# Two buffers instead of four for the gathered rows of a message-passing kernel

## The chip, the cores and the metric

The kernel runs on one core of a Trainium2 chip. The metric is the device time of one launch in microseconds (us). Before the change it is 5778.92 us, the median of three runs (5755.6 to 5812.79).

## The reference

One layer of a graph network with 12,500 nodes and 400,000 edges, all in float32, edges sorted by destination. A node has 160 numbers: 64 scalars `s` and 32 three-vectors `v`. Cut to what matters:

```python
h_s = s @ lin1_ws * a * _inv(S_IN)                  # per node
h_v = einsum('nci,cd->ndi', v, lin1_wv) * a * ...
hid = silu(edge_scalars @ fc_w1 * _inv(R))          # per edge
w1, w2, w3, w4, w5 = split(hid @ fc_w2 * ..., ...)  # 224 weights per edge
es, ev = h_s[edge_src], h_v[edge_src]               # the gather
m_s1 = w1 * es * e0;   m_s2 = w4 * einsum('eci,ei->ec', ev, e1) * ...
m_v1 = (w2 * es)[:, :, None] * e1;  m_v2 = w3 * ev * e0;  m_v3 = w5 * cross(ev, e1) * ...
agg  = segment_sum(concat(...), edge_dst)           # per node again
out  = layernorm(x + gate(self_connection + agg @ lin2))
```

## The kernel before

**Stages.** A first stage (to about 115 us in the profile) computes the node table `h = [h_s, h_v]` and stores it as `h_tab` in HBM, 640 bytes a row. The long middle stage runs over the edges. A tile is 128 edges, one in each partition; there are 3125 tiles. Five tiles make a block (625 of them), whose messages go to a window of 32 destination nodes. Twenty tiles make a chunk, which is worked off in five steps of four tiles, called quads here. There are 782 steps: 780 of four tiles, then one of four and one of one tile. After a short end nothing is left: the node outputs are worked off between the steps.

**One step `n`** of the loop at the end (line 607 on) does this:

- `hide(n + 1)`: at every chunk's first step, SyncE loads the edge scalars `es` of the chunk (line 278, 320 KB in two transfers, two buffers); TensorE then multiplies them into `ph` (L290) and ScalarE applies SiLU into `hid` (L292).
- `gather(deep, ...)`: GpSimd issues one indirect DMA for each of the four tiles (L299). Each brings 128 rows of `h_tab`, 80 KB, into a quarter of the tile `hg`. The addresses are a column of `idx`, which SyncE loads for 125 tiles at a time (L466), as it does the edge attributes `eat` (L468).
- `weights`: TensorE makes the 224 weights of each edge in PSUM, `pw` (L311), in two buffers.
- `products`: VectorE multiplies `pw` by `hg` into `pr`: one instruction at L319, then three at L328. L319 is the first that needs the gathered rows, the last L328 the last one that reads them. `pr` has two buffers.
- Still on VectorE: one finished block is added to the node sums `acc` (L387), and the selection matrices of a later block are made, `oh` (L338) and `sel` (L341).
- `now`: for a pair of blocks that was finished in an earlier step, TensorE transposes (L369), ScalarE copies (L370), and for every eighth block TensorE applies the second linear map (L378).
- `sum_up` of the step before: TensorE sums the messages of four tiles into `pa` with 16 small matmuls (L357). A pair of finished blocks is copied out by ScalarE (L361).

**Order.** TensorE, VectorE, ScalarE and GpSimd execute in the order in which this loop is written; SyncE's order is a scheduler's. [...] GpSimd has nothing to do in the middle stage but gathers, so it runs ahead of the others, until no buffer of `hg` is free.

**Where the buffers come from.** `hg` is the only tile of the pool `deep`, and a pool with `bufs=k` hands out k buffers in turn. So the first gather of step n waits until the last L328 of step n-4 has read that buffer:

```python
    def gather(pool, idx):
        hg = pool.tile([P, Q, D], F32, name="hg")
        for t, i in enumerate(idx):
            nc.gpsimd.indirect_dma_start(
                out=hg[:, t, :], out_offset=None, in_=h_tab,
                in_offset=bass.IndirectOffsetOnAxis(ap=i, axis=0))
        return hg
```

A buffer of `hg` is 4 tiles of 160 float32, 2.5 KB in each partition. A loop at the end of the program that repeats the work for wide blocks uses the same pool; on these data it runs zero times.

Of the kernel before, what the change touches and what calls it, by code (L numbers as in the profile page):

```python
# [64 lines left out]
def gnn_kernel(  # L65
# [76 lines left out]
    with tc.tile_pool(name="nodes", bufs=2) as nodes, tc.tile_pool(  # L142
        name="nodes_ps", bufs=8, space=PSUM
# [310 lines left out]
    with tc.tile_pool(  # L454
        name="fin", bufs=1
    ) as fin, tc.tile_pool(name="edge", bufs=2) as edge, tc.tile_pool(
        name="deep", bufs=4
    ) as deep, tc.tile_pool(name="pw_ps", bufs=2, space=PSUM) as pw_ps, tc.tile_pool(
        name="pa_ps", bufs=2, space=PSUM
    ) as pa_ps, tc.tile_pool(name="misc_ps", bufs=2, space=PSUM) as misc_ps:  # L460
# [268 lines left out]
```

## Time and profile before

| | |
|---|---|
| median of three runs | 5778.92 us |
| the profiled execution | 5669.53 us, span of its instructions 5667.7 us |
| mean granted TensorE clock in it | 0.816 |
| middle stage | 781 steps from 120.8 to 5626.3 us, 7.05 us a step |
| TensorE / VectorE / GpSimd / ScalarE busy | 74% / 47% / 54% / 14% of the span |
| gathers (L299) | 3125, median 946 ns each, with 0.30 us between two of a quad |

A row of the table of groups names a source line, the engine, the operation, what it writes and reads, how often, its busy time and the mean duration, and then how long the engine stood idle just before such instructions and what ended most of that. A row of the list of waits says: engine and line, what it waited for, total us, times, longest us. A row of the timeline says: start, duration, engine, line, what it writes and reads, how many instructions were merged, and in brackets the idle time before and what ended it. "issue" there is time in which nothing that the profile shows was waited for; "remote" is an end that the profile can't assign to an instruction. The end of a matmul in the trace is modelled, not observed, so the "busy" of TensorE isn't a measure of how full it is.

### The profile page before, as it was taken

How to read it: one execution, taken by the hardware profiler on the slowest of the kernel's cores; microseconds unless marked ns; L12 is line 12 of the kernel's file. 1: busy time of each engine (PE TensorE's matmuls, PEld its weight loads, DVE VectorE, ACT ScalarE, POOL GpSimd, SP SyncE). 2: the span in 40 equal slices, each digit the busy share in tenths (PEclk: the TensorE clock that was granted, in tenths of full speed). 3: DMA queues.
4: the chain of work that ended last, by engine and by line, in shares of the span. 5: the costliest groups of instructions: out<-in, count | busy, mean ns of one | idle time of the engine just before them, and what ended most of it. 6: DMA issues, size and time to landing. Idle time of an engine off the chain costs nothing.

```text
span 5667.7 us, 89792 instructions
## 1 busy us (share of the span) xinstructions
PE 4182.8 (74%) x36179; PEld 2227.6 (39%) x36179; DVE 2642.3 (47%) x5628; ACT 809.3 (14%) x1639; POOL 3051.9 (54%) x3134
## 2 busy tenths in 40 slices
PE   6777777767777767777777777777776767777776
PEld 5334433333344434334333333433333433434343
DVE  4444444444444444444444444444444444444444
ACT  0111111111111111111111111111111111111111
POOL 3555555555555555555555555555555555555553
PEclk7788887888888878888888788887887888888787
DMA  6222222222222222222222222222222322232221
GB/s 172 68 72 73 72 72 66 73 74 65 76 76 67 74 68 74 74 70 74 72 74 73 63 76 69 73 77 68 75 72 63 82 67 73 71 79 69 68 69 46
DMA packets 232392, 416.39 MB, mean 73 GB/s; under 512 B 64580, under 2 KB 160592, under 8 KB 231713
## 3 DMA queue, kind: packets, MB, share of 16 engines
q0 software_dynamic: 150000, 256.20, 17.3%
q1 hardware_dynamic: 65972, 142.43, 9.9%
q10 hardware_dynamic: 15994, 11.93, 0.8%
q8 instruction: 285, 4.67, 0.3%
q14 instruction: 141, 1.16, 0.1%
HBM read 394.32 MB, written 16.00 MB: 72 GB/s over the span
## 4 chain that ended last, share of the span: by engine, by line
PE 31%; another core or an unknown queue 8%; issue 6%; DVE 3%; ACT 3%; DVEq 0%; DMA 0%; POOL 0%; ACTq 0%; POOLq 0%
PE pa L357 13%; PE pw L311 6%; PE ph L290 4%; PE po L378 3%; PE pt L369 2%; DVE pr L328 2%; ACT tt L370 1%; PE pa L348 1%; ACT hid L292 1%; DVE pr L319 0%; PE pp L406 0%; PE psc L510 0%; ACT L292 0%; DVEq L582 0%
## 5 line engine op out<-in xcount | busy, mean ns | idle before, releaser
L299 POOL DMA_INDIRECT hg<-h_tab,idx x3125 | 3029.5, 969 | 2562.8 <-DVE pr L328 962.0
L357 PE MATMUL pa<-pr,sel 128*32 128x192 f32 x25000 | 1813.8, 395 | 312.7 <-issue 298.8
L319 DVE TENSOR_TENSOR pr<-pw,hg 128x512 f32<-128x512 f32 x782 | 539.1, 689 | 2648.7 <-remote 1400.2
L357 PEld LDWEIGHTS pa<-pr,sel 128*32 128x32 f32 x25000 | 888.3, 127 | 1060.3 <-issue 768.8
L328 DVE TENSOR_TENSOR pr<-pw,hg 128x384 f32<-128x384 f32 x2346 | 1158.2, 549 | 5.7 <-issue 4.9
L311 PE MATMUL pw<-w,hid 64*128 64x224 f32 x6250 | 990.0, 429 | 48.3 <-issue 38.8
L369 PE MATMUL pt<-ident,sa 128*96 128x128 f32 x1250 | 317.8, 344 | 814.6 <-ACT tt L370 418.6
L311 PEld LDWEIGHTS pw<-w,hid 64*128 64x128 f32 x6250 | 645.2, 219 | 585.8 <-issue 530.2
L341 DVE TENSOR_TENSOR sel<-oh,eat 128x640 f32<-128x640 f32 x625 | 517.8, 828 | 168.2 <-PE pw L311 51.2
L290 PE MATMUL ph<-es,w 128*128 128x512 f32 x940 | 552.0, 673 | 10.8 <-issue 8.3
L369 PEld LDWEIGHTS pt<-ident,sa 128*96 128x96 f32 x1250 | 124.7, 144 | 1000.5 <-ACT tt L370 496.0
L361 ACT COPY sa<-pa 128x384 f32<-128x384 f32 x313 | 149.5, 478 | 2085.0 <-PE pa L357 1042.7
L292 ACT ACTIVATE hid<-ph 128x512 f32<-128x512 f32 (+1 forms) x470 | 247.0, 526 | 1242.9 <-PE ph L290 855.1
L378 PE MATMUL po<-tt,l 96*96 96x256 f32 (+1 forms) x1738 | 401.7, 383 | 9.6 <-issue 8.7
L378 PEld LDWEIGHTS po<-tt,l 96*96 96x96 f32 x1738 | 274.5, 164 | 127.1 <-issue 47.6
L370 ACT COPY tt<-pt 96x256 f32<-96x256 f32 x626 | 229.3, 366 | 588.0 <-PE pt L369 361.1
L290 PEld LDWEIGHTS ph<-es,w 128*128 128x128 f32 x940 | 165.8, 219 | 198.1 <-issue 184.7
L406 PE MATMUL pp<-ident,acc 96*128 96x96 f32 x196 | 44.9, 325 | 239.6 <-DVE acc L387 218.9
L338 DVE TENSOR_TENSOR oh<-rel,iota 128x160 f32<-128x160 int16 x625 | 196.3, 314 | 0.0
L382 ACT COPY os<-po 96x512 f32<-96x512 f32 (+1 forms) x79 | 45.6, 577 | 714.9 <-PE po L378 485.1
L387 DVE TENSOR_TENSOR acc<-acc,os 96x64 f32 x625 | 132.7, 212 | 12.6 <-ACT os L382 7.9
L406 PEld LDWEIGHTS pp<-ident,acc 96*128 96x128 f32 x196 | 23.8, 170 | 273.3 <-issue 187.5
(61 smaller groups left out, 794.7 us busy)
## 6 DMA issues: line engine op xcount, KB each, us to landing
es<-in_es_t_dram SPq DMA_DIRECT2D x312, 320.0 KB
hg<-h_tab,idx POOLq DMA_INDIRECT x3125
h_tab<-ht ACTq DMA_DIRECT2D x8, 960.0 KB
xt<-in_x_dram SPq DMA_DIRECT2D x24, 320.0 KB
out_dram<-y SPq DMA_DIRECT2D x24, 320.0 KB
eat<-in_ea_dram SPq DMA_DIRECT2D x25, 250.0 KB
xv<-in_xv_t_dram SPq DMA_DIRECT2D x25, 187.5 KB
xs<-in_xs_t_dram SPq DMA_DIRECT2D x25, 125.0 KB
```

Of the source, the lines that this page charges most:

```text
L290: nc.tensor.matmul(ph[:k, c], w1[:k, :k], es[:k, t0 * P + c0 * P:t0 * P + c1 * P], start=True, stop=True)
L292: nc.scalar.activation(hid[:k, c], ph[:k, c], AF.Silu, scale=1.0 / math.sqrt(64))
L299: nc.gpsimd.indirect_dma_start(out=hg[:, t, :], out_offset=None, in_=h_tab, in_offset=bass.IndirectOffsetOnAxis(ap=i, axis=0))
L311: nc.tensor.matmul(pw[:, t, :NWT], hid[r, c * P:(c + 1) * P], w2[r], start=True, stop=True)
L319: nc.vector.tensor_mul(pr[:, :n, 6 * V:10 * V].rearrange("p t (k c) -> p t k c", k=2), pw[:, :n, :2 * S].rearrange("p t (k c) -> p t k c", ...
L328: nc.vector.tensor_mul(bass.AP(tensor=full.tensor, offset=full.offset, ap=[full.ap[0], full.ap[1], [step * V, 3], [1, V]]), pw[:, :n, None ...
L338: nc.vector.tensor_tensor(oh, r[:, :, None].to_broadcast([P, TB, W]), iota[:, None, :].to_broadcast([P, TB, W]), op=OP.is_equal)
L341: nc.vector.tensor_mul(sel, oh[:, :, None, :].to_broadcast([P, TB, 4, W]), e[:, :, :, None].to_broadcast([P, TB, 4, W]))
L357: nc.tensor.matmul(pa[k * W:(k + 1) * W], sel[:, t, k], a, start=start, stop=stop)
L369: nc.tensor.transpose(pt[:, half, b], sa[:, b, half * V3:(half + 1) * V3], ident)
L370: nc.scalar.copy(tt[:, half, :, at_b:at_b + nb].rearrange("c k b n -> c b k n"), pt[:, half, :nb].rearrange("c b (k n) -> c b k n", k=4))
L378: nc.tensor.matmul(po[:, k, :nb], l2[:, terms[to, part, half]], tt[:, half, part, :nb], start=(n == 0), stop=(n == len(of) - 1))
```

## The change

The pool of the gathered rows has two buffers instead of four. Nothing else is edited.

```diff
     with tc.tile_pool(
         name="fin", bufs=1
     ) as fin, tc.tile_pool(name="edge", bufs=2) as edge, tc.tile_pool(
-        name="deep", bufs=4
+        name="deep", bufs=2
     ) as deep, tc.tile_pool(name="pw_ps", bufs=2, space=PSUM) as pw_ps, tc.tile_pool(
```

The first gather of step n now waits for the last L328 of step n-2. In the built program the instructions of TensorE, VectorE, ScalarE and GpSimd stand in the same order as before. On GpSimd the waits are attached otherwise: before, each gather of a quad waited for the landing of the gather eight places earlier, and the quad's first one also for VectorE; now the first one carries all of this (four landings and VectorE), and the other three wait for nothing. On SyncE, eight of the 25 loads of `idx` stand behind the `es` load of one more chunk, and a few loads of `idx`, `eat`, `xt` and stores of the output have changed places.

## The prediction

> **What bounds the kernel now.** I read the page's busy shares first, then the groups of L299 and L319, then the list of waits, then the timeline of GpSimd and VectorE side by side.
>
> ```profile
> PE 4182.8 (74%) x36179; PEld 2227.6 (39%) x36179; DVE 2642.3 (47%) x5628; ACT 809.3 (14%) x1639; POOL 3051.9 (54%) x3134
> ...
> L299 POOL DMA_INDIRECT hg<-h_tab,idx x3125 | 3029.5, 969 | 2562.8 <-DVE pr L328 962.0
> ```
>
> ```profile
> DVE pr L319 <- remote: 1400.2, 267, 19.1
> ...
> DVE pr L319 <- PE pw L311: 784.7, 285, 10.1
> ...
> DVE pr L319 <- DMA hg<-h_tab,idx: 16.9, 2, 16.6
> ```
>
> ```profile
> PEld pa L357 <- DVE pr L328: 23.6, 48, 1.2
> ...
> PE pa L357 <- DVE pr L328: 6.6, 17, 0.9
> ```
>
> No engine is full by its busy share. The waits say who is last: VectorE's product (L319) waits 2,649 us in all, for TensorE or for "remote", and for gathered rows only twice, both at the start. TensorE in turn hardly waits for products: 30 us in all (23.6 + 6.6). So in the middle stage TensorE's own chain sets the pace of 7.05 us a step. VectorE follows it with slack, and GpSimd follows VectorE: 962.0 us of its idle time end with the release of a buffer at L328. The doubt is "remote", 1400.2 us: could these be gathers? The timeline answers:
>
> ```profile
> 2498.34 0.95 POOL L299 DMA_INDIRECT hg<-h_tab,idx  x1 [3.96 <-DVE pr L328]
> ...
> 2503.35 0.95 POOL L299 DMA_INDIRECT hg<-h_tab,idx  x1 [0.31 <-issue]
> ...
> 2513.20 0.94 POOL L299 DMA_INDIRECT hg<-h_tab,idx  x1 [5.16 <-DVE acc L387]
> ```
>
> ```profile
> 2511.46 1.47 DVE L328 TENSOR_TENSOR pr<-pw,hg 128x384 f32<-128x384 f32 x3
> ...
> 2513.69 0.69 DVE L319 TENSOR_TENSOR pr<-pw,hg 128x512 f32<-128x512 f32 x1 [0.62 <-PE pw L311]
> 2514.37 1.49 DVE L328 TENSOR_TENSOR pr<-pw,hg 128x384 f32<-128x384 f32 x3
> ...
> 2524.64 0.69 DVE L319 TENSOR_TENSOR pr<-pw,hg 128x512 f32<-128x512 f32 x1 [7.49 <-remote]
> ...
> 2530.28 0.69 DVE L319 TENSOR_TENSOR pr<-pw,hg 128x512 f32<-128x512 f32 x1 [2.25 <-PE pw L311]
> ...
> 2538.71 0.69 DVE L319 TENSOR_TENSOR pr<-pw,hg 128x512 f32<-128x512 f32 x1 [3.33 <-PE pp L406]
> ```
>
> The product that ends at 2512.93 (2511.46 + 1.47) frees a buffer, and 0.27 us later GpSimd starts the quad for the product four steps on, at 2538.71. Counting back, the quad of 2498.34 belongs to the product at 2524.64, which waited 7.49 us for "remote"; its rows had been ordered by 2503.04, some 20 us earlier. So "remote" isn't the gather. The prefetch is far deeper than its latency needs.
>
> [...]
>
> ```profile
> 117.74 0.95 POOL L299 DMA_INDIRECT hg<-h_tab,idx  x1 [0.30 <-issue]
> ...
> 120.78 0.69 DVE L319 TENSOR_TENSOR pr<-pw,hg 128x512 f32<-128x512 f32 x1 [16.60 <-DMA hg<-h_tab,idx]
> ```
>
> From 118.69 to 120.78 are 2.1 us; the second product, which started at 125.39 behind a gather row that ended at 123.69, gives 1.7.
> [...] I use the trace's 1.7 to 2.1.
> [...] Gathers here take 940 to 1591 ns with a median of 946 and a mean of 969[...].
> [...] The trace shows half-clock stretches (0.50 in 2519.82 to 2530.05 us, 1.00 in 2482.28 to 2495.92)[...].
>
> **The change, part by part.**
>
> *1. The wait at the first gather: release by step n-2 instead of n-4.* Behind it on GpSimd are only later gathers; who waits for them is L319, and everything behind that on VectorE. From release to usable rows a quad takes 0.27 us, plus 4.70 (three times 1.25 and 0.95, the quad of 2498.34), plus 1.7 to 2.1: **6.7 to 7.1 us**. What is available is the time from the end of one product to the start of the second after it, on average two steps less one product: 2 x 7.05 - 2.17 = 11.9 us. Checked in the window: the product at 2524.64 would have its quad started at 2513.20 and usable at 2520.0, 4.6 us early; that at 2530.28 would be served behind it (start 2518.2, usable 2525.0), 5.3 early; that at 2538.71, released at 2526.82, would be usable at 2533.9, 4.8 early. GpSimd's own rate is no bound: 5.0 us a quad against 7.05.
>
> The mean isn't enough, since steps are uneven. Taking the interval for all 780 pairs from the timeline of L319 and L328: median 11.8, lowest twentieth below 7.9, lowest hundredth below 6.0, least 3.7 us (the last step of one tile). The tight ones are where TensorE's backlog has let three products come close, as at 668.01, 670.25 and 674.84: the last starts only 4.64 us after the first has ended at 670.20. Passing all products through the two-buffer rule in order, with the durations of this trace, makes 18 of them late with 1.7 us of landing, 26 with half a us more; by 2.8 us at most, **15 to 27 us** together. If VectorE's idle time before the next products takes this back, 2 to 3 us remain at the end; if nothing does, 15 to 26. I take most of it as regained, because TensorE needs a product only one step later, behind the next `pw` and the sums of the step before, and its waits for products are the 30 us above: **+4 us**, ends 0 and +27.
>
> *2. The waits gathered on the quad's first instruction.* Three or four more semaphore waits, whose rows on GpSimd's queue are 17 ns each: at most 0.07 us a quad, 53 us in all, beside 2,563 us of GpSimd idle. If it came after the release it would add 0.07 to the 6.7, inside the half us tried above. Without waits the other three gathers keep their 0.30 us spacing, as the first eight did at 115 to 123 us, which had none either. **0**.
>
> *3. SyncE's order.* Eight `idx` loads stand one `es` load later. That for group 7 now follows the load for chunk 39, which can start when chunk 37's scalars have been read (step 188); its first gather is that of step 217, released at step 215: 27 steps, some 190 us, cover a 62.5 KB load. Each `idx` load also waits until the gathers of the group before last have been issued, now two steps (14 us) later, with `eat`, `xt` and `es` queued behind it. The next `es` load is free to start only about five steps after the last one (35 us), so its own wait covers this. If that cover failed, 25 times 14 us would be on SyncE, and `ph` would be late. **0**, upper bound a few us each.
>
> *4. Below nothing?* No instruction leaves TensorE, VectorE or ScalarE, gathers start at the same releases as before, so DMA traffic falls in the same places. I see no gain beyond the clock's wandering.
>
> Sum: 5669.5 + 4 = 5673.5 us for the profiled execution, +0.07%. It lies 1.9% below the median of the runs shown (5778.92), so I carry the ratio over: **5783 us**.
>
> **The rivals.**
> - *Two quads are too few* (slower). If a quad needs 2 us more than 6.7[...], GpSimd's 5.0 + 2 us reach the step of 7.05 and lateness no longer heals: the same pass gives 55 us (idle taken back) to 222 us, with 2.5 us 435 or more. With 1 us it is still only 4 to 46, so it decides from about 2 us on. Against it: the gathers' narrow durations, and the two landings seen. [...] Middle: +140 us, **5920**.
> - *The gathers collide less* (faster). Later fetches might fall beside fewer other transfers, and TensorE's clock might be granted more. The windows of 1000 us differ between 0.81 and 0.83, so 1% is conceivable: **5720**. Against it: point 4.
> - *The change does nothing, because no more than two quads were ahead anyway*: **5779**. Ruled out as a reading by the 20 us above, but its time is the forecast's.
>
> **How the numbers follow.** Within 1% is about what a measurement here can tell from no change (the three runs spread by 1%). Forecast and the last rival 0.77, too few quads 0.17, of which nearly all above 1%, faster 0.06. So faster 0.06, same 0.77, slower 0.17. The range: the forecast with 0 to +27 us and the runs' own spread of half a per cent gives 5745 to 5830; I stretch it up to 5860 for the near end of the slower case (5834 to 6000).
>
> **What will show it.** Right: L319's wait for `hg` stays under some 40 us; the gathers' rows end some 4 to 6 us before the product's start, less landing, instead of 20; GpSimd's idle ends about as before, at L328; TensorE's waits for products stay near 30 us. Wrong: L319 waiting for `hg` by hundreds of us, gathers longer than 1 us on average, or `ph` waiting for `es`.

## The result, and the profile after

| | before, four buffers | after, two buffers |
|---|---|---|
| median of 12 runs | 5790.27 us | 5798.77 us |
| range | 5755.60 to 5812.79 us | 5774.58 to 5819.40 us |
| ratio, with its 95% interval | | 1.0018 [0.9997, 1.0038] |
| profiled execution | 5669.53 us | 5819.40 us |

The change cost about 0.2%, 8.5 us, and the interval touches no change. The two profiled executions must not be compared by their spans: that of the kernel before lies 1.5% below the lowest of its own 12 timed runs, and that of the kernel after is the highest of its. What can be compared is who waited for whom. One later execution of the two-buffer kernel took 11758 us, at a granted clock of 0.54; the ratio of its group below leaves it out. The waits of L319 and of GpSimd in the profile after:

```profile
DVE pr L319 <- remote: 1562.7, 287, 8.2
POOL hg L299 <- DVE pr L328: 1050.3, 299, 5.4
...
DVE pr L319 <- PE pw L311: 711.0, 261, 9.7
...
DVE pr L319 <- DMA hg<-h_tab,idx: 34.8, 9, 14.6
```

VectorE waited for gathered rows 34.8 us instead of 16.9, of which 14.6 are the first product. Five products take nearly all of the rest, 3.8 us each; one of them, with the gathers of its quad:

```profile
1541.63 0.68 DVE L319 TENSOR_TENSOR pr<-pw,hg 128x512 f32<-128x512 f32 x1
...
1548.77 0.69 DVE L319 TENSOR_TENSOR pr<-pw,hg 128x512 f32<-128x512 f32 x1 [3.77 <-DMA hg<-h_tab,idx]
```

```profile
1541.85 0.95 POOL L299 DMA_INDIRECT hg<-h_tab,idx  x1 [3.52 <-DVE acc L387]
...
1544.36 1.46 POOL L299 DMA_INDIRECT hg<-h_tab,idx  x1 [0.30 <-issue]
```

The product before last had started at 1539.40, only 2.23 us ahead of the last one, and released the buffer at 1541.59; the rows were usable 7.19 us later. All five look like this: two products 2.1 to 2.2 us apart, then 7.2 to 7.3 us from the release to the next start. In each, one gather of the quad took 1.2 to 1.5 us. Of the 210 gathers over 1.1 us in this profile, 191 ran beside VectorE's L341, and one beside no VectorE instruction.

TensorE's waits for products stayed as small as they were:

```profile
PE pa L357 <- DVE pr L328: 5.3, 15, 0.9
PEld pa L357 <- DVE pr L328: 18.2, 36, 1.2
```

The timeline of GpSimd, and then of VectorE, shows the shorter lead:

```profile
2494.47 0.95 POOL L299 DMA_INDIRECT hg<-h_tab,idx  x1 [0.30 <-issue]
2500.62 0.95 POOL L299 DMA_INDIRECT hg<-h_tab,idx  x1 [5.20 <-DVE acc L387]
...
2504.37 0.95 POOL L299 DMA_INDIRECT hg<-h_tab,idx  x1 [0.30 <-issue]
```

```profile
2498.87 1.49 DVE L328 TENSOR_TENSOR pr<-pw,hg 128x384 f32<-128x384 f32 x3
...
2502.83 0.69 DVE L319 TENSOR_TENSOR pr<-pw,hg 128x512 f32<-128x512 f32 x1 [1.19 <-PE pw L311]
...
2512.21 0.69 DVE L319 TENSOR_TENSOR pr<-pw,hg 128x512 f32<-128x512 f32 x1 [6.20 <-remote]
```

A product ends at 2500.36, and 0.26 us later GpSimd starts the quad for the product after the next, at 2512.21. Its last row ends at 2505.32, 6.9 us before that product. Over all products this lead is 6.8 us in the median, where it was 20.6. It still exceeds the 1.7 us of landing (the time from the end of a gather's row to the start of a product that waited for it: 2.1 and 1.7 us at the two such products of the profile before), except at a handful of products.

What "remote" is, the trace itself tells: all 267 such waits of L319 in the profile before, and all 287 in the profile after, were ended by a semaphore that only TensorE's instructions raise.

### The profile page after: what moved, and what is told of

It is laid out like the page before. It is cut to its first block, busy times and chain, and to the rows that moved or that the text cites. A ratio compares the mean times of both kernels' runs of the same rounds, so it can differ in the third digit from the quotient of the medians.

```text
span 5817.6 us, 90561 instructions
## 1 busy us (share of the span) xinstructions
PE 4182.1 (72%) x36179; PEld 2230.7 (38%) x36179; DVE 2641.9 (45%) x5628; ACT 807.1 (14%) x1639; POOL 3055.7 (53%) x3134
## 4 chain that ended last, share of the span: by engine, by line
PE 26%; another core or an unknown queue 8%; issue 8%; POOL 4%; ACT 3%; DVE 2%; DMA 1%; DVEq 0%; POOLq 0%; ACTq 0%
PE pa L357 11%; PE pw L311 5%; POOL hg L299 4%; PE ph L290 3%; PE po L378 3%; PE pt L369 2%; DVE pr L328 1%; ACT tt L370 1%; PE pa L348 1%; ACT hid L292 1%; DMA hg<-h_tab,idx 1%; PE psc L510 0%; ACT L292 0%; ACT sa L361 0%
## 5 line engine op out<-in xcount | busy, mean ns | idle before, releaser
L357 PE MATMUL pa<-pr,sel 128*32 128x192 f32 x25000 | 1804.3, 396 | 292.4 <-issue 281.1
L319 DVE TENSOR_TENSOR pr<-pw,hg 128x512 f32<-128x512 f32 x782 | 539.6, 690 | 2746.9 <-remote 1562.7
L357 PEld LDWEIGHTS pa<-pr,sel 128*32 128x32 f32 x25000 | 889.7, 128 | 1033.6 <-issue 737.4
L328 DVE TENSOR_TENSOR pr<-pw,hg 128x384 f32<-128x384 f32 x2346 | 1159.6, 550 | 5.5 <-issue 4.6
L341 DVE TENSOR_TENSOR sel<-oh,eat 128x640 f32<-128x640 f32 x625 | 517.7, 828 | 208.5 <-PE pw L311 75.6
```

What stands on the lines that cost most here:

```text
L319: nc.vector.tensor_mul(pr[:, :n, 6 * V:10 * V].rearrange("p t (k c) -> p t k c", k=2), pw[:, :n, :2 * S].rearrange("p t (k c) -> p t k c", ...
L328: nc.vector.tensor_mul(bass.AP(tensor=full.tensor, offset=full.offset, ap=[full.ap[0], full.ap[1], [step * V, 3], [1, V]]), pw[:, :n, None ...
L341: nc.vector.tensor_mul(sel, oh[:, :, None, :].to_broadcast([P, TB, 4, W]), e[:, :, :, None].to_broadcast([P, TB, 4, W]))
L357: nc.tensor.matmul(pa[k * W:(k + 1) * W], sel[:, t, k], a, start=start, stop=stop)
```

## The experiments

**The chips.** The experiments ran on four chips, and the kernel before, byte for byte the same, has two quite different times on them. On two it took 5650.07 and 5646.96 us (medians), not far from the 5790 us of the result; these are called chips A here. On the other two it took 4218.01 and 4216.23 us; these are chips B. What makes them differ isn't known. Which kind a group of runs would meet couldn't be chosen, so several expectations name both.

**The kernel before once more (met B)**

> The kernel before, unchanged, for a second profile of it. Its first profiled execution took 5669.5 us, below all of its timed runs (5755.6 to 5812.8), while that of the two-buffer kernel took 5819.4. If the first profile was only an unusually quick execution: span 5750 to 5815 us, about 7.2 us a step, and VectorE's wait for TensorE and 'remote' as in the two-buffer profile. If instead the two profiles show a true difference of 2.6%: span near 5670 again.

Neither was found: 4219 us. So this became a profile of a chip B. Its busy shares and waits:

```profile
PE 3465.6 (82%) x36179; PEld 1994.9 (47%) x36179; DVE 2637.2 (63%) x5628; ACT 814.3 (19%) x1639; POOL 3094.3 (73%) x3134
...
L299 POOL DMA_INDIRECT hg<-h_tab,idx x3125 | 3071.9, 983 | 1077.8 <-issue 864.8
```

```profile
POOL hg L299 <- issue: 864.8, 2837, 0.3
DVE pr L319 <- DMA hg<-h_tab,idx: 754.9, 355, 7.3
...
DVE pr L319 <- PE pw L311: 523.9, 205, 14.9
```

The reading has turned round. "remote" is gone, L319 waits most for gathered rows, and GpSimd's idle time is mostly "issue", the 0.30 us between two gathers: of the other 213 us, 90 are its first wait, and it waits for VectorE only some 90 us in all. At 5.0 us a quad GpSimd is the floor of a step of 5.2 us. What has become faster is TensorE. Its timeline on chip A (the profile of before) and on chip B, at the message sums:

```profile
2505.84 0.68 PE L357 MATMUL pa<-pr,sel 128*32 128x192 f32 x9
2506.76 0.55 PE L357 MATMUL pa<-pr,sel 128*32 128x192 f32 x5 [0.24 <-issue]
2508.20 0.50 PE L357 MATMUL pa<-pr,sel 128*32 128x192 f32 x3 [0.90 <-issue]
2508.91 0.32 PE L357 MATMUL pa<-pr,sel 128*32 128x192 f32 x1 [0.21 <-issue]
2509.61 1.58 PE L357 MATMUL pa<-pr,sel 128*32 128x192 f32 x14 [0.38 <-issue]
```

```profile
2008.64 1.51 PE L357 MATMUL pa<-pr,sel 128*32 128x192 f32 x32
```

The same 32 instructions of one step (two for each of the 16 matmuls of the program) take 1.5 us on chip B; on chip A some of them start only every 0.7 us, with nothing waited for that the trace shows. Cutting L357's start times into sets of 32, 12.5% take over 4 us from the first start to the last in the profile before (10 to 15% in the profiles with two and three buffers on chips A), and none on chip B. Together the sets take 1840 us in the first and 1111 us in the second, which is half of the 1450 us between the two profiles; where the other half goes wasn't worked out. VectorE's instructions have the same durations on both (L319 689 ns on average).

**One buffer (met B)**

```diff
-        name="deep", bufs=4
+        name="deep", bufs=1
```

> One buffer of gathered rows instead of two or four. My theory (the depth costs nothing as long as release to usable rows, 6.7 to 7.1 us, fits into the time between the release and the next use): with one buffer the quad can only start after the last product has ended, so each step takes at least 6.7 to 7.1 plus the product's 2.17 us, 8.9 to 9.3 us, or 6950 to 7250 us for 782 steps, and in all 7200 to 7550 us (ratio 1.24 to 1.30). The wait of L319 for hg rises from 35 us to over 3500 us. Rival (gathered rows are never late, whatever the depth, because TensorE's chain sets the time): 5790 us, ratio 1.00. Rival[...]: over 7700 us, with the granted clock well below 0.8.

7390.94 us, within the range forecast from release, quad, landing and product; the step is 9.24 us on average and 8.87 in the median. The ratio on that chip is 1.75 [1.743, 1.757], since the kernel before takes 4218 us there.

```profile
DVE pr L319 <- DMA hg<-h_tab,idx: 4083.7, 702, 8.6
```

The price of a quad is thus right: release 0.27, quad 4.70, landing 1.72 and product 2.18 us (medians of this profile) are 8.87 us. The mean lies above it because landing has a tail: in a fifth of the waits the rows came over 2.5 us after the last gather's row had ended, at most 4.9. The rival that gathered rows are never late fell. The slower rival fell by its time (over 7700 us), though the granted clock did go down, to 0.75 from 0.91.

**Half of the message sums left out, with four and with two buffers (met B)**

```diff
-            nc.tensor.matmul(pa[k * W:(k + 1) * W], sel[:, t, k], a, start=start, stop=stop)
+            if k < 2 or stop:
+                nc.tensor.matmul(pa[k * W:(k + 1) * W], sel[:, t, k], a, start=start, stop=stop)
```

> Four buffers, but TensorE makes only the first two of the four message sums of each tile (except at the tile that ends a pair of blocks), so half of the matmuls of L357 are left out and the sums are incomplete. If TensorE sets the pace, this is much faster: 4700 to 5300 us, 5.6 to 6.4 us a step. If VectorE or the gathers set it: within 2% of 5790. GpSimd's floor is 5.0 us a quad, 3920 us for the steps.

> The same with half of L357's matmuls left out, and two buffers. My theory: two quads are enough only because the step is 7 us long. At a step of about 6 us, two steps less a product leave 9.8 us against 6.7 to 7.1 on average, with GpSimd at 5.0 of 6, so many more products are late: L319 waits 100 to 600 us for hg, and the kernel is slower than with four buffers by 0.5 to 6%. Rival (two buffers are enough at any pace that GpSimd can serve): the same time as with four within 0.4%, wait of L319 for hg under 50 us.

Four buffers: 4217.64 us, ratio 0.9996 [0.9985, 1.0008]. That nothing was gained doesn't show that TensorE has no part in the pace, because TensorE was not relieved. The sums with all of the matmuls (the kernel before on this chip), then with nearly half of them left out:

```profile
L357 PE MATMUL pa<-pr,sel 128*32 128x192 f32 x25000 | 1355.7, 358 | 243.8 <-DVE pr L328 239.1 <-DVE sel L341 3.0
```

```profile
L358 PE MATMUL pa<-pr,sel 128*32 128x192 f32 x13752 | 1344.4, 359 | 270.4 <-DVE pr L328 265.7 <-DVE sel L341 4.0
```

By the trace TensorE is busy with them as long, 1344 us against 1356: 25000 of 358 ns each add up to 8950 us and fit into 1356 us only side by side, and those left out had run beside the others. So this kernel stands in well for the kernel before. That GpSimd sets the pace on chip B rests on the waits in the profile of the kernel before on this chip, above, and on the clearing below.

Two buffers: 4519.88 us, 1.0705 [1.0664, 1.0746] to the kernel before, and 7.2% over the partner with four, a little above the 0.5 to 6% expected. This is the outcome of the prediction's slower rival, on the other kind of chip. The groups of GpSimd, first with four buffers, then with two:

```profile
L299 POOL DMA_INDIRECT hg<-h_tab,idx x3125 | 3073.9, 984 | 1091.3 <-issue 958.7 <-DVE pr L328 42.7 <-DMA hg<-h_tab,idx 35.7
```

```profile
L299 POOL DMA_INDIRECT hg<-h_tab,idx x3125 | 3042.8, 974 | 1394.7 <-issue 768.8 <-DMA hg<-h_tab,idx 160.9 <-DVE acc L388 158.3
```

GpSimd's idle time grew by 303 us while its busy time fell by 31, and the profiled span grew by 274 (the medians by 302). L319's wait for rows grew from 780.5 to 1126.9 us. The reckoning, an estimate from these durations: from the end of a quad's last row to the release of its buffer are 1.7 (landing) + 2.17 (product) + 0.27 = 4.1 us, while GpSimd works 5.3 us at the next quad; a product delayed by more than 1.1 us stops GpSimd, which as the engine that sets the pace has no idle time to regain it from. In the profiles GpSimd stood still for over 0.4 us 198 times with two buffers, 411 us in all, and 28 times, 52 us, with four.

**Two buffers again, and three (met A)**

The kernel after, and `bufs=3`.

> The two-buffer kernel, unchanged, beside the kernel before on the same chip. On the chip of the last four runs the kernel before takes 4218 us: none of L357's matmuls are slow there, and GpSimd's 5.0 us a quad is the floor of a 5.2 us step. My theory now: the depth costs nothing while TensorE makes the step 7 us, and costs time where GpSimd sets it. With two buffers GpSimd may start the next quad but one only after a product; from the quad's last row to that release are 1.7 (landing) + 2.17 (product) + 0.27 = 4.1 us, while GpSimd works 5.3 us at the next quad, so every delay of a product of over 1.1 us stops GpSimd and is not regained. Expected where the kernel before takes some 4220 us: ratio 1.05 to 1.09 (the pair with half the sums had 1.07), GpSimd busy 67 to 70%, its idle time behind VectorE 300 to 500 us. Where the kernel before takes some 5790 us: 0.998 to 1.005. Rival (two buffers are as good as four on any chip, and the 7% of the pair came from its missing sums): 1.00 in both.

> Three buffers. By the same theory GpSimd's slack behind a product is one quad more, 1.1 + 5.0 = 6.1 us, more than nearly every delay of a product: where the kernel before takes 4220 us, the ratio is 1.000 to 1.01; where it takes 5790, 1.00. Rival (each buffer less costs its share, half of the loss of two buffers): 1.03 to 1.04 on the first kind of chip.

Two: 5671.41 us against 5650.07, ratio 1.0035 [1.0018, 1.0052]. Three: 5663.18 us, 1.0015 [0.9997, 1.0032]. On chip A two buffers cost some tenths of a per cent, as in the result; for three the interval touches no change. The waits of L319 for rows in the profile with three buffers need care:

```profile
DVE pr L319 <- DMA hg<-h_tab,idx: 368.7, 87, 13.0
```

These are not late rows. For 85 of the 87 products the last gather's row had ended over 2.5 us before the start, in the median 13.8 us, and in 70 TensorE's own signal came within 0.15 us of it. The list puts a wait down to the semaphore that rose last; here that was most likely a later gather's.

**An additional gather for each quad (met A)**

```diff
-        hg = pool.tile([P, Q, D], F32, name="hg")
-        for t, i in enumerate(idx):
+        hg = pool.tile([P, Q + 1, D], F32, name="hg")
+        for t, i in [(Q + x, idx[0]) for x in range(1)] + list(enumerate(idx)):
```

> Four buffers, and ahead of each quad one more gather that nobody reads (into a fifth place of the tile, same addresses as the first): GpSimd needs 6.25 us a quad. Where the kernel before takes 4220 us, GpSimd sets the pace: 782 times 6.25 are 4890 us, with start and end 5020 to 5100 us, ratio 1.19 to 1.21. Where it takes 5790 us (7.05 us a step) the gather has room: ratio 1.00 to 1.01. Rival there (GpSimd or the DMA traffic does matter to that pace): over 1.02.

> Two buffers with the same additional gather. GpSimd now works 6.55 us at the next quad, against 4.1 us to the release: 2.4 us of slack instead of 1.1, so fewer delays stop it. Where the kernel before takes 4220 us: slower than four buffers with the additional gather by 1 to 4%, less than the loss without it (5 to 9%). Where it takes 5790 us, the passes through the traces gave 24 to 73 us of late products, mostly regained: ratio to four with the additional gather 1.000 to 1.012. Rival (the loss of two buffers is a fixed delay for each quad): the same number of microseconds as without the additional gather.

Four buffers: 6779.00 us, 1.1991 [1.1945, 1.2037]; two: 6756.56 us, 1.1963 [1.1910, 1.2015]. The two agree within their intervals, so depth did not matter here either. But that the gather costs 1129 us, 1.44 us a step, where GpSimd had room, was the rival's outcome and not mine. GpSimd isn't the bound in this profile: its rows are ready 24.9 us ahead in the median, it still waits for VectorE, and TensorE is the one that stretches. The list does show a wait for rows, but in 40 of its 42 cases (217 us) the last gather's row had ended over 2.5 us before:

```profile
DVE pr L319 <- DMA hg<-h_tab,idx: 234.9, 42, 16.1
```

```profile
L299 POOL DMA_INDIRECT hg<-h_tab,idx x3907 | 3767.1, 964 | 2945.4 <-issue 1152.9 <-DVE pr L328 1067.6 <-DVE acc L387 542.2
L357 PE MATMUL pa<-pr,sel 128*32 128x192 f32 x25000 | 2084.1, 408 | 600.0 <-issue 594.5 <-DVE pr L328 1.2
...
L357 PEld LDWEIGHTS pa<-pr,sel 128*32 128x32 f32 x25000 | 947.2, 131 | 1548.0 <-issue 1258.8 <-DVE oh L338 12.2 <-DVE pr L328 10.4
```

L357's idle time in "issue" grew from 298.8 to 594.5 us, and the sets of over 4 us from 12.5% to 20% (on this same chip 14% with two and with three buffers and no additional gather).

**GpSimd's time without the gather, and the gather's bytes without GpSimd (met B)**

```diff
         hg = pool.tile([P, Q, D], F32, name="hg")
+        nc.gpsimd.memset(idle, 0.0)      # idle: a constant tile [P, 1000]
```

```diff
                 hg = gather(deep, [index(t) for t, _, _ in tiles])
+                extra = deep.tile([P, D], F32, name="extra")
+                nc.scalar.dma_start(extra, h_tab[n * 15:n * 15 + P, :])
```

> Four buffers, and ahead of each quad GpSimd clears a scratch tile of 128 x 1000 numbers (about 0.9 us by the clearing of acc, 25088 numbers in 21.0 us; about 1.2 with the gap) in place of the additional gather, so GpSimd works nearly as long but no DMA is added. Where the kernel before takes some 5650 to 5790 us, an additional gather cost 1129 us although GpSimd had room. If GpSimd's own time is what costs: ratio 1.12 to 1.20. If it is the gather's DMA (its traffic or its descriptors): 0.995 to 1.02. Where the kernel before takes 4220 us, GpSimd sets the pace and the ratio is 1.15 to 1.20 in either case.

> Four buffers, and in each step one more transfer of 128 rows of h_tab, 80 KB, issued by ScalarE's queue, to a tile that nobody reads: the additional gather's bytes without GpSimd. Where the kernel before takes some 5650 to 5790 us: if the DMA traffic of the rows is what costs, ratio 1.12 to 1.20; if GpSimd's time or its descriptors, 0.995 to 1.03 (ScalarE's queue pays some 0.5 us a step for the issue, and is busy 14% of the time). Where the kernel before takes 4220 us: 1.00 to 1.02, unless the traffic delays the gathers' landing.

Clearing: 4818.94 us, 1.1425 [1.1401, 1.1450], 0.77 us a step, a little below the 1.15 to 1.20 expected. The clearing takes 0.95 us; GpSimd now waits for nobody (929 of its 938 us of idle time before gathers are "issue"), where before it had waited some 0.16 us a step. So on chip B, GpSimd's time is the kernel's time. Rows over ScalarE's queue: 4219.66 us, 1.0010 [0.9994, 1.0026]: their traffic costs nothing there. (The 0.5 us named for ScalarE's issue is near what the profile before shows: its 60 DMA issues took 0.54 us in the median.) Neither says anything of chip A.

**Two buffers and the clearing, once more (met A)**

> The two-buffer kernel, unchanged, once more beside the kernel before. Where the kernel before takes some 4220 us (two of the three chips so far that were not the first one): ratio 1.05 to 1.09 by the theory that GpSimd sets the pace there and has only 1.1 us of slack behind a product, with over 300 us of GpSimd idle behind VectorE; rival, that the 7% of the pair with half the sums came from the missing sums: 1.00 to 1.02. Where it takes 5650 to 5790 us: 1.000 to 1.006, as twice before.

> Four buffers and the clearing of a scratch tile ahead of each quad, once more. The clearing added 0.77 us a step where the kernel before took 4216 us. Where it takes 5650 to 5790 us: if what the additional gather cost there (1129 us) was GpSimd's own time, 300 to 900 us, ratio 1.05 to 1.16; if it was the gather's DMA, 0.995 to 1.02. Where it takes 4220 us: 1.14 again.

Two buffers: 5662.30 us, 1.0022 [1.0010, 1.0034], the third measurement of this on a chip A. The unchanged two-buffer kernel was therefore never measured on a chip B; its cost there is known only through the pair with half the sums. With 67.2 us, L319's wait for rows passed the 40 us that the prediction had named as its sign:

```profile
DVE pr L319 <- DMA hg<-h_tab,idx: 67.2, 23, 13.0
```

The clearing met none of the expectations: 5208.79 us, 0.9225 [0.9198, 0.9253], **faster** by 438 us. Its groups:

```profile
L359 PE MATMUL pa<-pr,sel 128*32 128x192 f32 x25000 | 1710.9, 382 | 160.5 <-issue 148.9 <-DVE sel L343 4.2 <-DVE pr L330 1.3
...
L299 POOL MEMSET idle<- 128x1000 f32 x782 | 742.7, 950 | 0.2
```

The message sums (now L359) wait 148.9 us in "issue" instead of 298.8, and the sets of over 4 us fell from 12.5% to 6% (15% with two buffers on this same chip). So GpSimd's own time is not supported as what the additional gather cost on chip A; the scratch tile also moved other tiles, which this doesn't separate. The same kernel is 8% faster than the kernel before on chip A and 14% slower on chip B.

## Why the prediction was right

- *Gathers are some 20 us early, "remote" isn't the gather.* Held: with the lead cut to 6.8 us, "remote" stayed (1562.7 us) and L319's wait for rows rose by 18 us. The semaphore behind "remote" is TensorE's. Less 1.7 us of landing, the lead is 5.1 us, inside the 4 to 6 that the prediction named.
- *6.7 to 7.1 us from release to usable rows.* Held: with one buffer, where every step pays it, the total was 7391 us within the 7200 to 7550 that it gives. It is the typical quad. The late products of the profile after had 7.2 to 7.3 us, because one gather was stretched, and landing alone went up to 4.9 us with one buffer; both tails lie outside the 6.7 to 7.1.
- *+4 us, ends 0 and +27.* The sign held; the size can't be told from +8.5 us in the result (interval -2 to +22). The two repetitions on chips A gave +21 and +15 us, with intervals clear of no change: inside the ends, nearer to "nothing is taken back". The tight spots were those foreseen, three products close together, but products that waited for rows were 9, 10 and 23 in the three profiles (2 before), where 18 to 26 were reckoned late, and the long waits took 3.8 us where 2.8 was the most reckoned. The reckoned number is soft: the pass done again, each quad with its own duration in the trace, gives 12 late products with 1.7 us of landing and 16 with half a us more, 12 to 18 us.
- *Most of it is regained.* Not shown. TensorE's waits for products did not grow (23.5, 22.0 and 31.0 us in the three profiles, 30.2 before), as the prediction said, yet time was lost. And three buffers, with no product late but the first two, took 13 us more in the median, with an interval that touches no change. So it stays open how much of the 15 to 21 us is late rows.
- *The waits gathered on the first gather, and SyncE's order: 0.* The first held where it can be seen: from release to first gather 0.27 us in both profiles, spacing in a quad 0.30 us. The rows of these waits were not 17 ns but mostly 43, some 0.09 us a quad where at most 0.07 was reckoned. SyncE's wait with an `idx` load rose from 48.4 to 119.0 us, as the step said it might, and no `ph` waited for `es`. They were not tried one at a time.
- *TensorE's own chain sets the pace.* That it was TensorE that came last holds for chips A. Whether this pace is its own is open: an additional gather stretched it by 20%, the clearing shortened it by 8%, and neither is work of TensorE. The forecast didn't depend on it, since the change leaves the number of gathers as it is, and their start follows the same releases.
- *Two quads are too few.* On chips A it did not come true; the pair on chip B shows that two can be too few, at 7%. The point named for it, a quad that takes 2 us more, comes by the same reckoning to a step that takes 2 us less: 5.0 us of GpSimd against a step of 5.2. Its middle of +140 us was the author's estimate.
- *Luck.* The prediction knew one kind of chip, and the kernels were compared on that kind. Two of the four later chips were of the other kind, where its premise of a 7 us step fails; had the comparison fallen there, the pair with half the sums says that the forecast would have been wrong by some 7%.

## What to carry to other kernels

How deep a prefetch must be is read from two intervals: from the release of a buffer to usable data, and from that release to the use of the same buffer, with its spread and not only its mean. Depth cost little (0.2 to 0.35%) while another engine set the pace; where the prefetching engine itself did, it cost 7% (in the pair with half the sums). By the reckoning above each delay beyond its slack is lost there, and one more buffer would add a whole quad of slack; three buffers were not run on such a chip, so the last isn't shown. Check a wait that the list puts down to a DMA against the age of its rows before believing it. So name the engine that sets the pace on the chip at hand: the same program may have another one on the next chip, and only a kernel before that was run beside it makes a ratio of use.

## What the runs showed of the hardware

- Two kinds of chip for one program: 4216 and 4218 us against 5647, 5650 and 5790 us. In the records of the first kind a set of 32 matmuls of L357 takes 1.2 to 2.9 us from its first start to its last. On the second kind half of the sets take no more than 1.7 to 2.1 us (with two to four buffers and nothing added), 10 to 15% take over 4, and the longest 9 to 20. The mean granted clock is 0.91 to 0.92 against some 0.82.
- A gather's row takes 0.95 us (median 946 ns in the profiles before and after). In the profile after, 210 of 3125 took over 1.1 us, 191 of them beside VectorE's L341; of the 1543 that ran beside no VectorE instruction, one did.
- On the second kind, one more gather a quad cost 1.44 us a step, and clearing a scratch tile on GpSimd gained 0.56 us a step. What stretched TensorE's sums with the additional gather (L357 busy 2084 us against 1814 in the profile before) stays open: its transfers, or where things lie. Both experiments also moved tiles in SBUF: the scratch tile shifts everything allocated after it by 4000 bytes a partition, the additional gather widens `hg` by 640. The timing and the placement weren't separated, and the bytes without GpSimd weren't tried on such a chip.
